# A linear-attention layer in four slots a chunk, with its convolution folded into the projection's weights, and one bias addition moved from ScalarE to VectorE

## The chip, the cores and the metric

The kernel runs on one core of one Trainium2 chip, as one launch. The metric is the time of that launch on the device, in microseconds (us); smaller is better. A core has five engines that run side by side, each through its own list of instructions in order: PE (TensorE, matrix products into PSUM banks), ACT (ScalarE), DVE (VectorE), POOL (GpSimd, which also issues the indirect DMAs) and SP (which issues the other DMAs). They wait for each other by semaphores.

## The reference

The program is a chain of sixteen layers on a tensor x of 16 sequences, 256 tokens and 128 features. Each layer adds its result on a normalized x to x. Two kinds of layer are touched by the change. The linear attention, cut to what it computes (`x` here is the normalized input):

```python
q = elu(x @ Wq.T) + 1
k = elu(x @ Wk.T) + 1
v = x @ Wv.T
kv = einsum('bhnd,bhne->bhde', k, v)              # 16 heads of 8
out = einsum('bhnd,bhde->bhne', q, kv)
den = maximum(einsum('bhnd,bhd->bhn', q, k.sum(tokens)), 1e-6)
xp = pad(x, one token on each side)
local = xp[:, :-2] * conv_w[:, 0] + xp[:, 1:-1] * conv_w[:, 1] + xp[:, 2:] * conv_w[:, 2] + conv_b
return (out / den + local) @ Wp.T + bp
```

The local layer (twice two of them in the program) is a windowed attention followed by a feed-forward part. Of the feed-forward part only its layer norm matters here: with h the token-shifted activations, `h = (h - mean) / sqrt(var + 1e-05) * lg + lb`, and `lb` is a bias for each feature.

## The kernel before

**Layout.** Features lie on the 128 partitions and tokens along the free dimension, all in 32-bit floats. The 4096 tokens are cut into 8 chunks of 512 tokens (two sequences each). x and the normalized activations h0 (the tile `ha`) stay in SBUF; the local layers hold a second tensor `hb`. Products go into 8 PSUM banks, which are handed out in turn, each by a `self.bank()`: a bank is used again once what was in it has been read.

**Slots.** `slots` (L1820) writes the order of a stage by hand. A stage is a list of steps; step i of chunk c is issued in slot `i + every * c`. Within a slot the later steps come first. The stage's own steps are followed by `last`, the first steps of the layer that comes next, which run on the chunks as they get done:

```python
for k in range((n - 1) * every + len(both)):
    ...
        for i in reversed(some):
            c, rest = divmod(k - i, every)
            if rest == 0 and 0 <= c < n and part < len(both[i]):
                both[i][part](c)
```

**The linear layer** (`linear`, L1966) has the steps: three of a norm (centre on PE; variance on PE and its root on ACT; scale on DVE), which chunks 0 to 4 have already behind them when the layer starts, since the layer before has run them ahead; `project` (q as one product 512 wide, k and v as eight 128 wide; then elu+1 of q and k: relu and exp on ACT, one step on DVE; and the convolution `l`, one step on ACT and two on DVE); `sums` (kv for two sequences, masked to its heads on DVE); `heads` (numerators and denominators on PE, then for each sequence a maximum, a reciprocal and a product on DVE); `join` (four transposes of o on PE, added to l on DVE); `out` (product with Wp, added to x on DVE). With `every=2` a chunk enters every second slot.

**What follows** is a mixture of experts. Its first steps (`Sending.steps`, L3644) are the `last` of the linear layer: three steps of a norm, `compare` (the gate's product on PE, comparisons on DVE), `choose` (DVE), `place` (small products on PE, DVE), `turn` (four transposes on PE, two copies on ACT) and `scatter`: eight indirect DMAs a chunk, issued by POOL, that write the rows of 128 tokens each to their places in DRAM (L3748). Before the first expert can run, SP fetches rows that these DMAs have written (L2165), together with the expert's weights (L2163). With `spread=False` all eight DMAs of a chunk are one step.

**The local layers' attention** (`local_attend`, L3363) has slots of its own, one for each half of a sequence's heads (32 in all; a chunk takes four). In each slot PE runs the score products, the products with v, transposes (`turn`), the value product, and two projections (`project`); ACT runs exponentials, copies out of PSUM, squares (sq), and the two small steps on `ss` that give each head's inverse length; DVE runs the four products `t` (rotary tables times the projections in PSUM), the minimum `pt` that masks the scores, the sum of squares and the division `ot`; POOL rotates (t<-t,t) and multiplies by the inverse lengths (t<-t,ss, 1.9 us). Three PSUM banks, tag "w", are shared by projections, transposes and the value product. Every fourth slot the output projection of a chunk (ps<-ot,w) comes in. Beside this `chunk_steps` (L3529) runs the norm of the feed-forward part for the chunks that are done: the four steps of `norm_of_half` (L3574), one a slot: centre, spread, scale (a DVE operation hb<-hb,w,nrs) and the bias (hb<-hb,w). In the slot of the bias, the steps are issued on DVE and ACT after `ot` and `ss` and before the `sq` and `t` of that slot's projection. The first layer of a local stage has one more step there for some chunks, the scale of the second layer's norm (ha<-ha,nrs on DVE).

**Helpers.** All operations go through short helpers, so that many have the line of a helper: `mm` L504 and `tr` L508 (PE), `act` L528 (ACT), `tt` L531, `ts` L538 and `stt` L543 (DVE), `gt` L534 (POOL).

Of the kernel before, what the change touches and what calls it, by code (L numbers as in the profile page):

```python
# [1649 lines left out]
class Fast(Net):  # L1650
# [313 lines left out]
            )  # L1964

    def linear(self, w):  # L1966
        x, h0 = self.x, self.ha
        nc = self.nc
        with ExitStack() as st:
            p = self.stage(st, "n2", 2)  # L1970
            qs, ks, kvs, os, ls = {}, {}, {}, {}, {}
            norm = [lambda c, i=i: self.norm_x_step(p, c, i) for i in range(3)]

            def elu1(ps, tag, bufs):
                e = p.tile([P, CH], F32, tag=tag, name=tag, bufs=bufs)
                self.act(e, ps, AF.Relu, scale=-1.0)
                self.act(e, e, AF.Exp, scale=-1.0)
                self.stt(e, ps, 0.0, e, ALU.max, ALU.add)
                return e

            def project(c):
                s = self.chunk(c)
                pq, pk, pv = self.bank(), self.bank(), self.bank()
                self.mm(pq, w["Wq"], h0[:, s])
                for t in range(4):
                    ht = h0[:, c * CH + t * P : c * CH + t * P + P]
                    self.mm(pk[:, t * P : t * P + P], ht, w["Wk"])
                    self.mm(pv[:, t * P : t * P + P], ht, w["Wv"])
                qs[c] = elu1(pq, "q", 3)
                k = elu1(pk, "k", 2)  # L1990
                v = p.tile([P, 4, P + 1], F32, tag="v", name="v")
                self.act(v[:, :, :P], pv.rearrange("p (t d) -> p t d", t=4), AF.Copy)
                nc.gpsimd.memset(v[:, :, P:], 1.0)
                ks[c] = k, v
                l = p.tile([P, CH], F32, tag="l", name="l", bufs=4)
                lb, hb = self.bt(l), self.bt(h0[:, s])
                self.act(l, h0[:, s], AF.Identity, scale=w["conv_w"][:, 1:2], bias=w["conv_b"])
                self.stt(lb[:, :, 1:], hb[:, :, : T - 1], w["conv_w"][:, 0:1], lb[:, :, 1:], ALU.mult, ALU.add)
                self.stt(lb[:, :, : T - 1], hb[:, :, 1:], w["conv_w"][:, 2:3], lb[:, :, : T - 1], ALU.mult, ALU.add)
                ls[c] = l  # L2000

            def sums(c):
                k, v = ks.pop(c)
                pkv = self.bank()
                for b in range(2):
                    for u in range(2):
                        t = 2 * b + u
                        self.mm(pkv[:, b * 129 : b * 129 + 129], k[:, t * P : t * P + P], v[:, t], start=u == 0, stop=u == 1)

                kv = p.tile([P, 2, P + 16], F32, tag="kv", name="kv")  # L2010
                src = pkv[:, :258].rearrange("p (b d) -> p b d", b=2)
                self.tt(kv[:, :, :P], src[:, :, :P], self.twice(self.k["blk8"]), ALU.mult)
                self.tt(kv[:, :, P:], src[:, :, P:].broadcast_to([P, 2, 16]), self.twice(self.k["blk8"][:, ::8]), ALU.mult)
                kvs[c] = kv

            def heads(c):
                q, kv = qs.pop(c), kvs.pop(c)
                o = p.tile([P, 4, P], F32, tag="o", name="o")
                for b in range(2):
# [4 lines left out]
                    src = pn[:, :288].rearrange("p (u d) -> p u d", u=2)  # L2024
                    rd = p.tile([P, 2, 16], F32, tag="rd", name="rd")
                    self.ts(rd, src[:, :, P:], 1e-6, ALU.max)
                    nc.vector.reciprocal(rd, rd)
                    self.tt(
                        o[:, 2 * b : 2 * b + 2].rearrange("p u (h d) -> p u h d", h=16),
                        src[:, :, :P].rearrange("p u (h d) -> p u h d", h=16),  # L2030
                        rd[:, :, :, None].broadcast_to([P, 2, 16, 8]), ALU.mult,
                    )
                os[c] = o

            def join(c):
                o, l = os.pop(c), ls[c]
                pt = self.bank()
                for t in range(4):
                    self.tr(pt[:, t * P : t * P + P], o[:, t])
                self.tt(l, l, pt, ALU.add)  # L2040

            def out(c):
                s = self.chunk(c)
                po = self.bank()
                self.mm(po, w["Wp"], ls.pop(c))
                self.stt(x[:, s], po, w["bp"], x[:, s], ALU.add, ALU.add)

            self.slots(NCH, *norm, project, sums, heads, join, out, last=self.lead(p), every=2)

    def mix(self, w):  # L2050

# [1536 lines left out]

    def local_ffn(self, w, z, hn, last):
# [261 lines left out]
```

## Time and profile before

| | us |
|---|---|
| median of 3 runs (4299.6, 4300.43, 4302.12) | 4300.43 |
| the profiled execution's own time | 4303.47 |
| its span in the profile | 4301.6 |
| linear layer: first projection to the first product of the experts | 1858.85 to 2011.31 |
| bias hb<-hb,w on ACT in the four attentions and feed-forward parts, one | 0.71 |

The busy shares over the whole span are 90% for PE, 61% DVE, 55% ACT and 49% POOL. In the timeline a line gives the start in us from the span's start, the duration in us, engine, source line, operation, output and inputs by tile names (buffer numbers left out), their shapes and how many equal ones are merged; in brackets stands the idle time before it and what ended it. A 32-bit matrix product shows as two records, so x2 is one product. Groups of instructions give the shortest, median and longest duration in ns. Windows give the busy time of each engine in a stretch, and behind them the clock that was granted to PE (1 is full) and the share of DMA engines in use.

### The profile page before, as it was taken

To read this page: it belongs to the slowest core of one execution; us is meant where nothing else is said; L and a number is where in the kernel's file an instruction comes from. 1 tells how busy PE (TensorE), PEld (TensorE's weight loads), DVE (VectorE), ACT (ScalarE), POOL (GpSimd) and SP (SyncE) were. 2 spreads that over 40 slices of the span, in tenths; PEclk is the share of its full clock that TensorE was granted. 3 is DMA by queue.
4 is the path that set the end of the run, shared out by engine and by line. 5 is a ranking of instruction groups with operands and counts; after the bars stand their busy time and mean duration, and the time that the engine had idled before them with its cause. 6 is when DMAs were issued, how large, how long until landed. Compare 5 with 4: busy or idle time off the path is not lost. (4 is left out here: it accounts for less than half of the span.)

```text
span 4301.6 us, 74012 instructions
## 1 busy us (share of the span) xinstructions
PE 3881.4 (90%) x28998; PEld 2210.2 (51%) x28998; DVE 2620.8 (61%) x4423; ACT 2369.4 (55%) x4821; POOL 2123.8 (49%) x1776
## 2 busy tenths in 40 slices
PE   7999999998899999985989879987999899899978
PEld 3555465465455466554955469543333343455333
DVE  4775576364577377464346633646888698386474
ACT  6665466555766466553456634454565544674432
POOL 4663465232565166226433334557988698421251
PEclk9999999988999999997999979998999999999989
DMA  1800000000000000004910068000000000000000
GB/s 60 339 2 1 11 2 1 19 1 1 20 1 2 3 2 1 1 6 147 321 60 15 18 213 272 18 18 16 1 1 1 3 0 1 15 2 18 6 0 21
DMA packets 78407, 176.45 MB, mean 41 GB/s; under 512 B 12607, under 2 KB 39109, under 8 KB 77921
## 3 DMA queue, kind: packets, MB, share of 16 engines
q1 hardware_dynamic: 65568, 148.40, 10.0%
q0 software_dynamic: 9120, 18.51, 1.2%
q8 instruction: 231, 3.78, 0.4%
q10 hardware_dynamic: 3360, 4.72, 0.3%
q14 instruction: 128, 1.04, 0.1%
HBM read 118.28 MB, written 54.20 MB: 40 GB/s over the span
## 5 line engine op out<-in xcount | busy, mean ns | idle before, releaser
L528 ACT ACTIVATE pt<-ps 128x512 f32<-128x512 f32 x640 | 339.7, 600 | 314.4 <-PE ps L504 313.1
L504 PE MATMUL ps<-hb,w 128*128 128x512 f32 (+1 forms) x960 | 464.4, 617 | 8.8 <-issue 3.3
L504 PE MATMUL ps<-w,hb 128*128 128x512 f32 (+2 forms) x896 | 405.5, 574 | 26.3 <-DVE t L531 20.4
L534 POOL TENSOR_TENSOR t<-t,t 128x512 f32<-128x512 f32 x256 | 319.6, 1270 | 161.5 <-DVE t L531 101.5
L531 DVE TENSOR_TENSOR t<-ps,tab 128x512 f32<-128x512 f32 x512 | 317.6, 681 | 84.9 <-ACT sq L528 81.5
L534 POOL TENSOR_TENSOR t<-t,ss 128x1024 f32<-128x1024 f32 x128 | 243.6, 1903 | 218.6 <-ACT ss L528 217.4
L504 PEld LDWEIGHTS ps<-hb,w 128*128 128x128 f32 (+1 forms) x960 | 180.0, 192 | 271.7 <-issue 239.8
L528 ACT ACTIVATE qkt<-ps 128x512 f32<-128x512 f32 x256 | 140.5, 595 | 309.6 <-PE ps L508 309.0
L531 DVE TENSOR_TENSOR ot<-ps,rd 128x512 f32<-128x512 f32 (+2 forms) x224 | 143.1, 639 | 254.3 <-ACT rd L528 254.3
L531 DVE TENSOR_TENSOR u<-u,ps 128x384 f32<-128x384 f32 (+1 forms) x206 | 121.8, 595 | 287.4 <-PE ps L508 186.1
L534 POOL TENSOR_TENSOR nsq<-ha 128x512 f32<-128x512 f32 x112 | 123.2, 1100 | 316.9 <-ACT ha L528 304.8
L504 PEld LDWEIGHTS ps<-w,hb 128*128 128x128 f32 x896 | 156.3, 193 | 184.4 <-issue 115.0
L504 PE MATMUL ps<-nsq,ct 128*128 128x512 f32 x368 | 203.0, 635 | 36.0 <-POOL nsq L534 32.1
L504 PE MATMUL ps<-ot,w 128*128 128x512 f32 x448 | 215.4, 615 | 16.8 <-DVE ot L531 9.0
L2199 POOL DMA_INDIRECT back<-y,x x142 | 139.1, 980 | 183.8 <-ACT y L528 68.0
L504 PE MATMUL ps<-u,w 128*128 128x512 f32 (+1 forms) x448 | 218.1, 611 | 8.3 <-POOL u L534 8.3
L504 PE MATMUL ps<-xt,w 128*128 128x128 f32 x1704 | 221.0, 280 | 1.5 <-ACT xt L528 1.5
L528 ACT ACTIVATE u<-ps,w 128x512 f32<-128x512 f32 x160 | 107.8, 685 | 183.2 <-PE ps L504 180.6
L531 DVE TENSOR_TENSOR pt<-pt,w 128x1024 f32<-128x1024 f32 (+1 forms) x96 | 181.1, 1886 | 42.7 <-ACT pt L528 42.7
L504 PEld LDWEIGHTS ps<-xt,w 128*128 128x128 f32 x1704 | 204.8, 194 | 2.9 <-ACT xt L528 2.9
L3748 POOL DMA_INDIRECT rows<-out,idx x128 | 125.9, 983 | 155.0 <-ACT out L528 105.7
L528 ACT ACTIVATE nrs<-ps,ct 128x512 f32<-128x512 f32 x208 | 139.8, 684 | 98.9 <-PE ps L504 93.1
(367 smaller groups left out, 9302.6 us busy)
## 6 DMA issues: line engine op xcount, KB each, us to landing
w<-in_moe_x SPq DMA_DIRECT2D x142, 533.0 KB
rows<-t SPq DMA_DIRECT2D x64, 520.0 KB
x<-rows SPq DMA_DIRECT2D x142, 65.0 KB
w<-in_local_f SPq DMA_DIRECT2D x8, 659.5 KB
y<-back ACTq DMA_DIRECT2D x16, 256.0 KB
y<-back SPq DMA_DIRECT2D x16, 256.0 KB
w<-in_local_f SPq DMA_DIRECT2D x4, 658.5 KB
back<-y,x POOLq DMA_INDIRECT x142
```

Of the source, the lines that this page charges most:

```text
L504: self.nc.tensor.matmul(out, lhsT, rhs, start=start, stop=stop)
L528: self.nc.scalar.activation(out, in_, func, **kw)
L531: self.nc.vector.tensor_tensor(out, a, b, op)
L534: self.nc.gpsimd.tensor_tensor(out, a, b, op)
L2199: nc.gpsimd.indirect_dma_start(views[i], bass.IndirectOffsetOnAxis(ap=x[:, C : C + 1].bitcast(I32), axis=0), y, None, bounds_check=2 * NT ...
L3748: nc.gpsimd.indirect_dma_start(views[(c * 2 + k) * 4 + t], bass.IndirectOffsetOnAxis(ap=idx[:, k, t : t + 1], axis=0), out[:, k, t], None,)
```

## The change

In the linear layer `every` goes from 2 to 4, and the elu's last DVE step becomes a step of its own, `grown`, a slot behind `project`. The convolution is no longer computed: the product with Wp of the shifted inputs is taken with three weight matrices, Wp scaled by each of the three taps, which are made once behind chunk 0's `grown`, together with a bias that holds `Wp conv_b + bp`. `join` now begins the output product of the chunk in its bank, with one product 512 wide and four 255 wide, and copies the transposed o out of PSUM on ACT; `out` adds the product of that copy to the same bank. In `heads` one reciprocal serves both sequences. The scatters of a chunk are four steps of two DMAs. In `norm_of_half`, which all four local layers use, the bias is added on DVE instead of ACT.

```diff
     def linear(self, w):
...
-            p = self.stage(st, "n2", 2)
+            one = self.stage(st, "n1", 1)
+            p = self.stage(st, "n2", 2)
...
+            taps = one.tile([P, 3, P], F32, tag="taps", name="taps")
+            bias = one.tile([P, 1], F32, tag="bias", name="bias")
+
+            def prepare():
+                for j in range(3):
+                    self.ts(taps[:, j], w["Wp"], w["conv_w"][:, j : j + 1], ALU.mult)
+                pb = self.bank()
+                self.mm(pb[:, :1], w["Wp"], w["conv_b"])
+                self.tt(bias, pb[:, :1], w["bp"], ALU.add)
...
-                qs[c] = elu1(pq, "q", 3)
-                k = elu1(pk, "k", 2)
+                made = []
+                for ps, tag in ((pq, "q"), (pk, "k")):
+                    e = p.tile([P, CH], F32, tag=tag, name=tag, bufs=3)
+                    self.act(e, ps, AF.Relu, scale=-1.0)
+                    self.act(e, e, AF.Exp, scale=-1.0)
+                    made.append((ps, e))
...
-                l = p.tile([P, CH], F32, tag="l", name="l", bufs=4)
-                lb, hb = self.bt(l), self.bt(h0[:, s])
-                self.act(l, h0[:, s], AF.Identity, scale=w["conv_w"][:, 1:2], bias=w["conv_b"])
-                self.stt(lb[:, :, 1:], hb[:, :, : T - 1], w["conv_w"][:, 0:1], lb[:, :, 1:], ALU.mult, ALU.add)
-                self.stt(lb[:, :, : T - 1], hb[:, :, 1:], w["conv_w"][:, 2:3], lb[:, :, : T - 1], ALU.mult, ALU.add)
-                ls[c] = l
+                ks[c] = made, v
+
+            def grown(c):
+                made, v = ks[c]
+                for ps, e in made:
+                    self.stt(e, ps, 0.0, e, ALU.max, ALU.add)
+                qs[c] = made[0][1]
+                ks[c] = made[1][1], v
+                if c == 0:
+                    prepare()
...
             def heads(c):
...
+                for b in range(2):
+                    self.ts(rd[:, b], srcs[b][:, :, P:], 1e-6, ALU.max)
+                nc.vector.reciprocal(rd, rd)
...
             def join(c):
-                o, l = os.pop(c), ls[c]
-                pt = self.bank()
+                o = os.pop(c)
+                hs = h0[:, self.chunk(c)]
+                pt, po = self.bank(), self.bank()
+                self.mm(po, taps[:, 1], hs, stop=False)
+                for b in range(2):
+                    at = b * T
+                    self.mm(po[:, at + 1 : at + T], taps[:, 0], hs[:, at : at + T - 1], start=False, stop=False)
+                    self.mm(po[:, at : at + T - 1], taps[:, 2], hs[:, at + 1 : at + T], start=False, stop=False)
                 for t in range(4):
                     self.tr(pt[:, t * P : t * P + P], o[:, t])
-                self.tt(l, l, pt, ALU.add)
+                ot = p.tile([P, CH], F32, tag="ot", name="ot")
+                self.act(ot, pt, AF.Copy)
+                pos[c] = po, ot
 
             def out(c):
                 s = self.chunk(c)
-                po = self.bank()
-                self.mm(po, w["Wp"], ls.pop(c))
-                self.stt(x[:, s], po, w["bp"], x[:, s], ALU.add, ALU.add)
-
-            self.slots(NCH, *norm, project, sums, heads, join, out, last=self.lead(p), every=2)
+                po, ot = pos.pop(c)
+                self.mm(po, w["Wp"], ot, start=False)
+                self.stt(x[:, s], po, bias, x[:, s], ALU.add, ALU.add)
+
+            self.slots(NCH, *norm, project, grown, sums, heads, join, out, last=self.lead(p, spread=True), every=4)
...
     def norm_of_half(self, pool, bank, w, s):
...
-            lambda: self.act(s, s, AF.Identity, bias=w["lb"]),
+            lambda: self.ts(s, s, w["lb"], ALU.add),
```

More of the change, by code (lines that the diff above doesn't have):

```diff
@@ L1969, in linear @@
         with ExitStack() as st:
+            one = self.stage(st, "n1", 1)
             p = self.stage(st, "n2", 2)
-            qs, ks, kvs, os, ls = {}, {}, {}, {}, {}
+            qs, ks, kvs, os, pos = {}, {}, {}, {}, {}
             norm = [lambda c, i=i: self.norm_x_step(p, c, i) for i in range(3)]
[L1974 to L1979, printed above, removed]
+            taps = one.tile([P, 3, P], F32, tag="taps", name="taps")
[6 more added lines that the diff above has]
+                self.tt(bias, pb[:, :1], w["bp"], ALU.add)
             def project(c):
@@ L1993, in project @@
                 nc.gpsimd.memset(v[:, :, P:], 1.0)
-                ks[c] = k, v
-                l = p.tile([P, CH], F32, tag="l", name="l", bufs=4)
-                lb, hb = self.bt(l), self.bt(h0[:, s])
-                self.act(l, h0[:, s], AF.Identity, scale=w["conv_w"][:, 1:2], bias=w["conv_b"])
-                self.stt(lb[:, :, 1:], hb[:, :, : T - 1], w["conv_w"][:, 0:1], lb[:, :, 1:], ALU.mult, ALU.add)
-                self.stt(lb[:, :, : T - 1], hb[:, :, 1:], w["conv_w"][:, 2:3], lb[:, :, : T - 1], ALU.mult, ALU.add)
-                ls[c] = l
+                ks[c] = made, v
[7 more added lines that the diff above has]
+                    prepare()
             def sums(c):
@@ L2018, in heads @@
                 o = p.tile([P, 4, P], F32, tag="o", name="o")
+                rd = p.tile([P, 2, 2, 16], F32, tag="rd", name="rd")
+                srcs = []
                 for b in range(2):
@@ L2023, in heads @@
                         self.mm(pn[:, u * 144 : u * 144 + 144], q[:, t * P : t * P + P], kv[:, b])
[L2024 to L2027, printed above, removed]
+                    srcs.append(pn[:, :288].rearrange("p (u d) -> p u d", u=2))
+                for b in range(2):
+                    self.ts(rd[:, b], srcs[b][:, :, P:], 1e-6, ALU.max)
+                nc.vector.reciprocal(rd, rd)
+                for b in range(2):
                     self.tt(
                         o[:, 2 * b : 2 * b + 2].rearrange("p u (h d) -> p u h d", h=16),
-                        src[:, :, :P].rearrange("p u (h d) -> p u h d", h=16),
-                        rd[:, :, :, None].broadcast_to([P, 2, 16, 8]), ALU.mult,
+                        srcs[b][:, :, :P].rearrange("p u (h d) -> p u h d", h=16),
+                        rd[:, b, :, :, None].broadcast_to([P, 2, 16, 8]), ALU.mult,
                     )
@@ L2035, in join @@
             def join(c):
-                o, l = os.pop(c), ls[c]
-                pt = self.bank()
+                o = os.pop(c)
+                hs = h0[:, self.chunk(c)]
+                pt, po = self.bank(), self.bank()
+                self.mm(po, taps[:, 1], hs, stop=False)
+                for b in range(2):
+                    at = b * T
+                    self.mm(po[:, at + 1 : at + T], taps[:, 0], hs[:, at : at + T - 1], start=False, stop=False)
+                    self.mm(po[:, at : at + T - 1], taps[:, 2], hs[:, at + 1 : at + T], start=False, stop=False)
                 for t in range(4):
                     self.tr(pt[:, t * P : t * P + P], o[:, t])
-                self.tt(l, l, pt, ALU.add)
+                ot = p.tile([P, CH], F32, tag="ot", name="ot")
+                self.act(ot, pt, AF.Copy)
+                pos[c] = po, ot
             def out(c):
                 s = self.chunk(c)
-                po = self.bank()
-                self.mm(po, w["Wp"], ls.pop(c))
-                self.stt(x[:, s], po, w["bp"], x[:, s], ALU.add, ALU.add)
-            self.slots(NCH, *norm, project, sums, heads, join, out, last=self.lead(p), every=2)
+                po, ot = pos.pop(c)
+                self.mm(po, w["Wp"], ot, start=False)
+                self.stt(x[:, s], po, bias, x[:, s], ALU.add, ALU.add)
+            self.slots(NCH, *norm, project, grown, sums, heads, join, out, last=self.lead(p, spread=True), every=4)
     def mix(self, w):
```

## The prediction

> **What bounds the kernel now.** I read the page first, for where TensorE (PE), the engine with 90% of the span, has holes; then windows around the changed stages; then the timelines there, engine by engine. The chain of waits covers only the last 6% of the span, far behind the change, so it says nothing here.
>
> ```profile
> span 4301.6 us, 74012 instructions
> ...
> PE   7999999998899999985989879987999899899978
> ...
> POOL 4663465232565166226433334557988698421251
> ```
>
> A slice is 107.5 us. The 5 in PE's row is slice 19, 1936 to 2043 us: the end of the linear layer. The slices from 110 to 1860 us, where the four local layers are, show 8 and 9. So the two edits meet different bounds.
>
> The linear layer, by windows (PE, PEld, DVE, ACT, POOL, clock, DMA), then its ends on POOL and PE:
>
> ```profile
> 1859.00:1922.00 63.00, 52.38 (x288) 37.06 (x287) 46.24 (x112) 33.83 (x59) 4.81 (x10) 0.95 0.01 1
> 1922.00:1981.00 59.00, 38.41 (x238) 25.78 (x237) 52.61 (x211) 29.41 (x56) 42.82 (x46) 0.87 0.20 61
> 1981.00:2011.00 30.00, 0.63 (x4) 0.35 (x4) 0.42 (x3) 0.00 (x0) 20.40 (x22) 0.50 0.22 70
> ```
> ```profile
> 1922.55 1.11 POOL L3748 DMA_INDIRECT rows<-out,idx  x1 [0.16 <-issue]
> ...
> 2006.83 0.97 POOL L3748 DMA_INDIRECT rows<-out,idx  x1 [0.31 <-issue]
> ```
> ```profile
> 2011.31 0.45 PE L508 MATMUL ps<-ct,x 128*128 128x128 f32 x1 [29.47 <-DMA x<-rows]
> ```
>
> In the last 30 us only POOL works: it issues the scatters that send the rows to the experts. There are 64, one each 1.27 us, 10.2 us a chunk; they begin at 1922.55 and end at 2007.8, and PE starts on the experts 3.5 us later. So the stage ends when POOL has issued its last scatter. Until 1950 DVE is 93% busy; projections of neighbouring chunks start 12.9 us apart (1921.83 and 1934.76).
>
> A local layer, one slot of the attention in which the bias is added:
>
> ```profile
> 616.70 0.69 DVE L531 TENSOR_TENSOR ot<-ps,rd 128x512 f32<-128x512 f32 x1 [2.30 <-ACT rd L528]
> 618.14 1.29 DVE L531 TENSOR_TENSOR t<-ps,tab 128x512 f32<-128x512 f32 x2 [0.76 <-ACT sq L528]
> ```
> ```profile
> 616.92 0.71 ACT L528 ACTIVATE hb<-hb,w 128x512 f32<-128x512 f32 x1
> ```
> ```profile
> 617.16 1.90 POOL L534 TENSOR_TENSOR t<-t,ss 128x1024 f32<-128x1024 f32 x1 [3.36 <-ACT ss L528]
> ```
> ```profile
> 619.67 1.09 PE L508 MATMUL ps<-ct,t 128*128 128x128 f32 x8
> 620.68 1.13 PE L504 MATMUL ps<-w,hb 128*128 128x512 f32 x2
> ```
>
> PE never rests here. But the value product at 620.68 writes the bank that the fourth product t (DVE, 618.14 to 620.62) has just read: PE is in time by nothing. Whatever delays t by more than 0.1 us delays PE.
>
> **The bias on DVE.** Removed: 32 ACT additions of 0.71 us (seven in each attention, one in each feed-forward part). Added: 32 DVE additions; the same operation in the performer gives the price, and its maximum a second one:
>
> ```profile
> L538 DVE TENSOR_SCALAR hb<-hb,w x8: 486/486/1151, 911.6 to 1046.8; 128x512 f32<-128x512 f32 x8
> ```
>
> The 1.15 us one began at 933.44 while a POOL operation ran (932.97 to 934.32); it ended 0.27 us after it. [...] This slot shows the same with another operation, in the cycles where the norm of a later chunk falls into it:
>
> ```profile
> 254.76 2.31 DVE L531 TENSOR_TENSOR ha<-ha,nrs 128x512 f32<-128x512 f32 x1
> ```
> ```profile
> 258.32 0.66 PE L508 MATMUL ps<-ct,t 128*128 128x128 f32 x4 [0.54 <-DVE t L531]
> 259.52 1.12 PE L504 MATMUL ps<-w,hb 128*128 128x512 f32 x2 [0.54 <-DVE t L531]
> ```
>
> It takes 0.68 us elsewhere, and here waits for POOL's product (254.62 to 256.53), as 20 of the 40 scale steps hb<-hb,w,nrs do: (61.5 us - 40 x 0.74) / 1.56 = 20. PE pays: from the slot's output projection to the next centring it takes 13.01 us without such an operation (608.63 to 621.64) and 14.39 with one (246.09 to 260.48), and the cycle of four slots grows from 34.35 (608.63 to 642.98) to 35.72 (322.01 to 357.73). That is 1.38 us a time, not won back.
>
> The moved addition stands in the same place, behind ot and ahead of the four t. It can issue at 617.31 (ot's start plus 0.61); POOL's product starts at 617.16, set by ACT's ss, which does not move. So it waits until 0.19 us ahead of that product's end (as ha did: 2.31 - 0.74 = 1.57 us after 254.76), 618.87, and ends at 619.36; t starts at 619.28 instead of 618.14. Queued behind it: four t, the minimum for the softmax, the sum of squares; PE waits for t. It costs 1.38 less the shorter operation (0.74 - 0.49), 1.13 us. Projections and t run only in five of a layer's seven bias slots, so 20 times. In six of these (chunks 1 to 3 in the first layer of each local stage) ha has waited already: the addition adds 0.41, or 0.77 if the POOL copy that follows goes first; I take 0.6. Sum: 14 x 1.13 + 6 x 0.6 = **+19.4 us**. The other twelve stand where no t follows: nothing, as DVE idles over half of those parts (feed-forward: 21.17 of 55 us). Bounds: never held, t starts 0.4 us earlier and the 0.08 us that PE waits now goes, 20 x -0.08 = -2; held at ha's price, 14 x 1.38 + 6 x 0.77 = +24.
>
> A rule speaks for this edit: the Trainium skill, Perfetto Trace Analysis, "Optimizing Scalar/DVE Operations", has an operation that Scalar or DVE can do run faster on DVE if a performance mode exists, unless DVE is saturated. By its word the edit is worth 32 x (0.49 - 0.71) = -7 us at most; the rows above decide against it.
>
> **The linear layer.** DVE loses, a chunk, two convolution steps (1.44 us start to start), the join (0.60) and one of two reciprocals (0.33): 12.9 - 2.4 = 10.5 us. ACT loses 0.80 and gains a 0.6 copy of ot. Prepare: three 128x128 scalings, some 0.2 us each, one tiny product, one tiny addition, before the first kv: hidden behind PE's first sums. PE gains the taps:
>
> ```profile
> 2899.13 1.88 PE L504 MATMUL ps<-ha,Wr 128*128 128x512 f32 x6
> 2900.85 1.45 PE L504 MATMUL ps<-ha,Wk 128*128 128x512 f32 x4
> ```
>
> One group there is a 512-wide product and two 255-wide: 1.72 us, so 0.86 and 0.43 each; the taps are 0.86 + 4 x 0.43 = 2.58 us a chunk. The slot with the projection now holds taps, transposes of o, projection and turn: 6.1 us of PE. The other three are chains. In us from a projection's start, by start-to-start times of the 1920 to 1936 timeline: projection 2.64, turn 0.44, out issued at 3.08, x on DVE at 4.18, q 4.84, k 5.44, sums on PE 0.84 behind k at 6.28, kv 7.45, choose 7.90, its 'both' done and place on PE at 9.62, mean 9.82, taps 10.76, transposes 13.34, next projection **13.8**. PE idles 1.4 us before sums and waits again for 'both'. With the norm of chunks 5 to 7 PE fills that: 6.28 + 0.97 + 0.94 + 0.86 + 0.98 + 0.20 + 0.94 + 2.58 + 0.43 = **14.2**. The fill: chunk 0 to 1 is 11.1 (sums at 5.04 as now, kv 6.27, heads 6.85 to 7.9, taps 2.7, transposes 0.43), then 13.1 and 13.4 (no turn yet). So the last projection stands at 11.1 + 13.1 + 13.4 + 13.8 + 3 x 14.2 = 94 us, plus 2 for the clock, which falls to 0.58 in the present fill (1873 to 1878) for idle gaps like these: 1858.85 + 96 = 1954.9, where it is 1934.76 now.
>
> The first scatter comes in the slot of the fourth projection, 37.6 + 4.9 = 42.5 us in (turn, then ACT's backlog, then a 0.5 us copy): 1901.4 instead of 1922.55. But a period of 14 is longer than POOL's 10.2, so POOL waits from chunk to chunk until chunk 4, turned beside the last projection: 1954.9 + 4.9 = 1959.8. From there chunks 4 to 7 need 4 x 10.2 = 40.8 us without a gap (5 is turned 13.8 us later, 6 and 7 follow each within 10): end at 2000.6, against 2007.8: **-7.2 us**. Scatters in pairs cost POOL nothing, as only memsets and three nsq (1.04 us) stand between. SP's order is unchanged; its row fetch follows POOL's end as now. Bounds: POOL never waiting after its first scatter, 1901.4 + 81.6 = 1983, -24.8; periods of 15.5 from the third on and another 4 us of half clock, +3.
>
> Sum: +19.4 - 7.2 = **+12.2 us**. The profiled execution took 4303.47 (span 4301.6, 1.9 around it), 3 above the median; the median becomes 4300.4 + 12.2 = **4312.6**.
>
> **The rivals.** First, other side: the addition is not held. It misses POOL's product by 0.15 us; if it starts first, POOL waits 0.49 us and nobody waits for POOL. Against it: ha and the scale step miss by the same 0.14 and are held all 20 times. Time 4300.4 - 7.2 - 1.6 = 4291.6; it decides once fewer than 7 of the 20 are held. Second: the linear chains overlap better, POOL runs saturated: 4300.4 + 19.4 - 24.8 = 4295. For it: PE's and DVE's work (11.9, 10.5) would allow 12; against it: the chain above. Third: the fold makes PE the bound, with the clock low: the linear layer 5 us slower, 4325. For it: PE's 2.6 us a chunk; against it: PE still idles 0.5 to 1.9 us in each period.
>
> **How the numbers follow.** Forecast 0.55 (own range 4304 to 4320), first rival 0.18, second 0.12, third 0.15. A measurement here tells 0.2% (8.6 us) from no change: below 4291.8, above 4309.0. Faster: six tenths of the first and a third of the second, 0.15. Same: the rest of these and a fifth of the forecast, 0.26. Slower: 0.59. The range 4291 to 4321 leaves out half of the first rival and two thirds of the third.
>
> **What would show it.** The bias row on DVE near 2.0 us where its price is 0.49; PE behind t 20 times more; the clean cycle at 35.5 instead of 34.35; the linear layer starting 19 us later. In it: projections 13.8 to 14.2 apart, first scatter 42 us behind the first projection, POOL gapless over the last four chunks, PE's hole of 29.5 us down to about 20. A bias row of 0.5 us, or scatters gapless from the first, would prove me wrong.

## The result and the profile after

The changed kernel takes 4320.58 us (median of 6 runs, 4314.88 to 4327.27), the kernel before 4301.45 us (6 runs): a ratio of 1.0042, 95% interval 1.0032 to 1.0052. It is 19.1 us slower. The profiled execution took 4322.03 us (span 4320.2), against 4303.47 (span 4301.6). The 18.6 us between the spans come about so: 21.3 were lost when the linear layer starts (first projection at 1880.17 instead of 1858.85), 20.0 of them in the local layers and 1.3 ahead of them; the linear layer gave 4.4 back (148.04 us from there to the experts' first product, instead of 152.46); another 1.7 were lost behind it. No edit touches the stretches that lost the 1.3 and the 1.7.

The page of the changed kernel, its span and its slices of 108 us:

```profile
span 4320.2 us, 74143 instructions
...
PE   7999999998899999997989879987999899899977
...
POOL 4654365232565166325433444457988699411251
```

Slice 19 of PE's row, the linear layer's, went from 5 to 7. The slices of the local layers still show 8 and 9, and the loss is in there: a digit of a tenth doesn't show the 3% by which a cycle grows. The group of the moved addition, which had x8 at a median of 486 ns, does:

```profile
L538 DVE TENSOR_SCALAR hb<-hb,w x40: 473/826/2044, 219.5 to 1836.1; 128x512 f32<-128x512 f32 x40
```

The timeline of one slot in the second local layer, the one the prediction showed, on DVE, POOL and PE:

```profile
624.41 0.69 DVE L531 TENSOR_TENSOR ot<-ps,rd 128x512 f32<-128x512 f32 x1 [2.30 <-ACT rd L528]
624.88 1.90 POOL L534 TENSOR_TENSOR t<-t,ss 128x1024 f32<-128x1024 f32 x1 [3.35 <-ACT ss L528]
625.02 2.04 DVE L538 TENSOR_SCALAR hb<-hb,w 128x512 f32<-128x512 f32 x1
626.98 2.47 DVE L531 TENSOR_TENSOR t<-ps,tab 128x512 f32<-128x512 f32 x4
628.31 0.66 PE L508 MATMUL ps<-ct,t 128*128 128x128 f32 x4 [0.47 <-DVE t L531]
629.51 1.12 PE L504 MATMUL ps<-w,hb 128*128 128x512 f32 x2 [0.54 <-DVE t L531]
```

POOL's product runs from 624.88 to 626.78; the addition is issued 0.14 us behind its start, stands for 2.04 us instead of 0.48, and ends 0.28 us after it. The first t starts 2.57 us behind ot, where it was 1.44. PE, which had waited for nothing here, waits 0.47 us for the transposes' input and 0.54 for the bank of the value product. The cycle of four slots grows from 34.35 to 35.44 us. These are the output projections that begin and end it, in the kernel before and in the changed one:

```profile
608.63 3.70 PE L504 MATMUL ps<-ot,w 128*128 128x512 f32 x8
642.98 3.70 PE L504 MATMUL ps<-ot,w 128*128 128x512 f32 x8
```

```profile
616.36 3.70 PE L504 MATMUL ps<-ot,w 128*128 128x512 f32 x8
651.80 3.70 PE L504 MATMUL ps<-ot,w 128*128 128x512 f32 x8
```

The linear layer by windows (PE, PEld, DVE, ACT, POOL, clock, DMA), and its ends on POOL and PE:

```profile
1880.00:1943.00 63.00, 54.59 (x296) 39.98 (x295) 33.41 (x106) 28.32 (x52) 12.62 (x17) 0.95 0.04 10
1943.00:2002.00 59.00, 53.57 (x293) 37.67 (x291) 40.58 (x152) 31.38 (x58) 38.21 (x42) 0.94 0.17 54
2002.00:2028.00 26.00, 3.80 (x24) 3.06 (x24) 7.84 (x38) 4.05 (x7) 17.39 (x18) 0.50 0.25 73
```

```profile
1925.37 1.10 POOL L3771 DMA_INDIRECT rows<-out,idx  x1 [24.14 <-DVE x L543]
2023.66 0.96 POOL L3771 DMA_INDIRECT rows<-out,idx  x1 [0.30 <-issue]
```

```profile
2028.21 0.45 PE L508 MATMUL ps<-ct,x 128*128 128x128 f32 x1 [14.76 <-DMA x<-rows]
```

DVE falls from 46.2 to 33.4 us in the first 63, PE rises from 52.4 (0.83) to 54.6 and in the second window from 38.4 to 53.6: the bound has moved from DVE to PE, which works 13.9 us of each of the last three periods of 14.6. The first scatter comes 45.2 us behind the first projection (63.7 before), the last 143.5 us behind it (148.0 before). Only 4.5 of the 18.5 us by which POOL starts earlier are left at its end: before chunk 4 it waits for the projections, which are now 13 to 14.6 us apart.

### The profile page after: what moved, and what is told of

It reads as the page before. It is cut to its first block, busy times and chain, and to the rows that moved or that the text cites. A ratio compares the mean times of both kernels' runs of the same rounds, so it can differ in the third digit from the quotient of the medians.

```text
span 4320.2 us, 74143 instructions
## 1 busy us (share of the span) xinstructions
PE 3902.2 (90%) x29080; PEld 2232.0 (52%) x29080; DVE 2639.1 (61%) x4427; ACT 2350.3 (54%) x4789; POOL 2127.0 (49%) x1776
## 5 line engine op out<-in xcount | busy, mean ns | idle before, releaser
L504 PE MATMUL ps<-hb,w 128*128 128x512 f32 (+1 forms) x960 | 464.5, 617 | 9.4 <-issue 3.3
L504 PE MATMUL ps<-w,hb 128*128 128x512 f32 (+2 forms) x896 | 406.2, 575 | 35.4 <-DVE t L531 28.4
L504 PEld LDWEIGHTS ps<-hb,w 128*128 128x128 f32 (+1 forms) x960 | 180.5, 193 | 273.2 <-issue 241.2
L504 PEld LDWEIGHTS ps<-w,hb 128*128 128x128 f32 x896 | 156.8, 194 | 196.2 <-issue 113.9
L504 PE MATMUL ps<-ot,w 128*128 128x512 f32 x464 | 222.9, 613 | 17.1 <-DVE ot L531 9.0
L504 PE MATMUL ps<-nsq,ct 128*128 128x512 f32 x368 | 200.3, 627 | 34.0 <-POOL nsq L534 29.1
L504 PE MATMUL ps<-u,w 128*128 128x512 f32 (+1 forms) x448 | 217.6, 609 | 8.0 <-POOL u L534 8.0
L504 PE MATMUL ps<-xt,w 128*128 128x128 f32 x1704 | 219.8, 279 | 1.5 <-ACT xt L528 1.5
L504 PEld LDWEIGHTS ps<-xt,w 128*128 128x128 f32 x1704 | 203.6, 193 | 2.8 <-ACT xt L528 2.8
```

The costliest lines, as they stand in the source:

```text
L504: self.nc.tensor.matmul(out, lhsT, rhs, start=start, stop=stop)
```

## The experiments

They ran on three chips (on which one the first comparison ran is not on record), where the kernel before takes 4325.4 us (the first four below), 4298.6 (the next four) and 4321.1 (the last four). Every ratio is to the kernel before on the same chip; it is estimated from all runs of both kernels and differs from the quotient of the medians by up to 0.0007. "Local" is the stretch from the first output projection of the first local layer to the first projection of the linear layer, "linear" the stretch from there to the experts' first product, both from the one profiled execution, which can lie some us off the median.

| kernel | median us | ratio, 95% interval | local us | linear us |
|---|---|---|---|---|
| before (first comparison) | 4301.45 | 1 | 1683.3 | 152.5 |
| changed (first comparison) | 4320.58 | 1.0042, 1.0032 to 1.0052 | 1703.3 | 148.0 |
| bias alone on DVE | 4347.70 | 1.0052, 1.0038 to 1.0066 | 1703.1 | 165.3 |
| linear layer alone | 4322.85 | 0.9994, 0.9985 to 1.0003 | 1683.1 | 158.0 |
| bias on DVE, early | 4312.61 | 0.9977, 0.9968 to 0.9986 | 1668.3 | 166.2 |
| slots without the fold | 4317.68 | 0.9981, 0.9972 to 0.9990 | 1684.5 | 157.1 |
| changed, bias early | 4289.90 | 0.9982, 0.9973 to 0.9991 | 1675.4 | 148.2 |
| no bias in the attention | 4294.25 | 0.9988, 0.9979 to 0.9997 | 1675.5 | 152.1 |
| fold without the slots | 4302.17 | 1.0004, 0.9995 to 1.0013 | 1685.0 | 152.5 |
| changed, bias early, x last | 4282.95 | 0.9970, 0.9958 to 0.9982 | 1671.9 | 144.8 |
| slots without fold, bias early | 4305.93 | 0.9964, 0.9953 to 0.9975 | 1668.6 | 155.1 |
| the same, x last | 4308.29 | 0.9970, 0.9960 to 0.9981 | 1675.5 | 156.0 |
| changed, bias early, no spreading | 4311.97 | 0.9981, 0.9970 to 0.9991 | 1668.6 | 161.7 |
| changed, bias early, x last, again | 4313.23 | 0.9980, 0.9970 to 0.9990 | 1671.9 | 158.9 |

On the first and the last of these three chips the linear layers are longer, on the first shown for the unchanged one too (165 instead of 152 us; more in the last section), so "linear" is compared within a group of four alone. "Local" moves by up to 7 us with PE's clock in the stage between the two local stages, which no edit touches; the cycles given below are free of that.

### One edit at a time

The bias alone, everything else as before:

```diff
-            lambda: self.act(s, s, AF.Identity, bias=w["lb"]),
+            lambda: self.ts(s, s, w["lb"], ALU.add),
```

> The kernel before, with the bias of norm_of_half on DVE and nothing else. If the addition is held by POOL's product and delays the four t (the forecast's mechanism), this edit alone costs all that the local part lost: +19 to +22 us (4321 to 4324), bias row near 2.04 us, cycle 35.44 instead of 34.35 us. If the loss belongs to the two edits together, or the bias is harmless, the time stays within 4299 to 4304. If the falls of PE's clock in the local part come from the longer waits, they are here at the same cycles (40.39 and 38.16 us); if they come with something else of the changed kernel, they are gone and the cost is near +16.

It costs 22 us (1.0052), and its local part is as long as the changed kernel's to 0.2 us. The addition's row is 473/827/2041 ns, the cycle 35.45 us, and the fall of PE's clock comes again (a cycle of 40.39 us in the second stage). So the loss is this edit's alone.

The linear layer alone is the changed kernel with that line put back:

> The changed kernel with the bias back on ACT. If the linear layer gains the 4.4 us that its two times show, 4297; cycles of the local part at 34.35 us again, first projection at 1858.9, first period 13.9 us. If the first period (13.9 us where 11.1 was forecast) was a lower clock left over from the local part, the first period falls to about 11 to 12 and the time to 4294. If the linear layer's gain was only bought with a pause that the bias gave it, 4301.

0.9994 with an interval that holds both 1 and the -4.4 us of the two profiles: not to be told from no change. Local is 1683.1 us again. The first period fell to 10.92 us, as the second theory had it, but the time did not follow, because on this chip the periods from the fifth projection on are 16.5 to 17.6 us instead of 14.6. Beside the unchanged linear layers of this group, 165.3 us with the bias alone and 166.2 with the early addition, its 158.0 is still 7 to 8 us shorter; in the profiled execution 3.8 us of that are lost ahead of the first local layer (first output projection at 180.27 us, at 176.49 and 176.48 in those two), where no edit works. The changed kernel with an early bias had a first period of 13.88 us without any loss in its local part, so what the longer stalls of the local part leave behind isn't its cause. PE's clock in this period itself is; the changed kernel, then this one:

```profile
1880.17:1894.04 13.87, 11.36 (x51) 8.87 (x50) 5.61 (x15) 2.96 (x6) 1.85 (x4) 0.75 0.02 1
```

```profile
1863.36:1874.28 10.92, 8.40 (x52) 6.62 (x51) 5.62 (x15) 2.95 (x6) 1.84 (x4) 1.00 0.03 2
```

PE is busy 2.96 us longer at a clock of 0.75, which is the whole difference. Why the clock fell in the one and not in the other is open.

### Where the addition stands

The same 32 additions on DVE, but in the attention issued ahead of `ot`:

```diff
+                    c, rest = divmod(m - 9, 4)
+                    if rest == 0 and 0 <= c < NCH - 1:
+                        steps[1][3]()
                     if within(m - 1, NTILE):
                         inverse(m - 1)
                         divide(m - 1)
...
-                for i in range(4):
+                for i in range(3):
                     if (c := due(6 + i)) is not None and c < NCH - 1:
```

> The kernel before with the same 32 additions on DVE, but in the attention each is issued ahead of ot instead of behind it, where DVE and POOL both rest. If it is the meeting with POOL's product that costs, the bias row falls to about 0.49 us, no t starts late, and the time is that of before: 4300 to 4303. If an added DVE operation in this slot costs wherever it stands (DVE's own length, or what DVE does behind it), 4311 to 4322.

Faster than before, by 10 us (0.9968 to 0.9986), where no change was expected. The same slot on DVE and POOL, and the group:

```profile
613.08 0.17 DVE L531 TENSOR_TENSOR ss<-ss,least 128x16 f32<-128x16 f32 x1
613.18 0.48 DVE L538 TENSOR_SCALAR hb<-hb,w 128x512 f32<-128x512 f32 x1
615.55 0.69 DVE L531 TENSOR_TENSOR ot<-ps,rd 128x512 f32<-128x512 f32 x1 [1.90 <-ACT rd L528]
616.39 0.69 DVE L531 TENSOR_TENSOR t<-ps,tab 128x512 f32<-128x512 f32 x1
```

```profile
616.01 1.91 POOL L534 TENSOR_TENSOR t<-t,ss 128x1024 f32<-128x1024 f32 x1 [3.35 <-ACT ss L528]
```

```profile
L538 DVE TENSOR_SCALAR hb<-hb,w x40: 473/480/1150, 216.1 to 1800.7; 128x512 f32<-128x512 f32 x40
```

The addition takes 0.48 us in a gap of DVE and ends 2.35 us before POOL's product begins. The first t starts 0.84 us behind ot, where it was 1.44 before the change and 2.57 with it. This shows that the meeting with POOL's product makes the addition dear, not the addition. The cycle is 33.96 us, 0.39 below that of before. That is so in the fourteen cycles without ha; the six with it stay as long as they were. Where it comes from shows on ACT, in the kernel before and then in this one:

```profile
616.57 0.45 ACT L528 ACTIVATE ss<-ss 128x16 f32<-128x16 f32 x2
616.92 0.71 ACT L528 ACTIVATE hb<-hb,w 128x512 f32<-128x512 f32 x1
617.53 1.06 ACT L528 ACTIVATE sq<-ps 128x512 f32<-128x512 f32 x2
618.49 0.45 ACT L528 ACTIVATE pu<-ps 128x128 f32<-128x128 f32 x2
```

```profile
615.43 0.45 ACT L528 ACTIVATE ss<-ss 128x16 f32<-128x16 f32 x2
615.78 1.06 ACT L528 ACTIVATE sq<-ps 128x512 f32<-128x512 f32 x2
616.73 0.45 ACT L528 ACTIVATE pu<-ps 128x128 f32<-128x128 f32 x2
```

Before, two things stood behind the addition on ACT: sq, which t waited 0.76 us for, and the copies pu, which begin 1.92 us behind ss there and 1.30 us here. PE's products of that slot take 1.96 us from the first to the transposes before (617.71 to 619.67), 1.76 here (616.57 to 618.33); the rest of the 0.39 us are two steps of PE behind t, 0.08 and 0.10 us shorter. To see whether it is ACT's addition and nothing else, the attention's additions were left out on both engines:

```diff
-                for i in range(4):
+                for i in range(3):
                     if (c := due(6 + i)) is not None and c < NCH - 1:
```

> The kernel before without the addition of lb in the four attentions, on either engine (chunks 0 to 6; the one in the feed-forward part stays). If the 0.39 us a cycle that the early addition won is ACT's 0.71 us, which stood between ss and the sq that t's next work waits for, the cycle is 33.96 us here too and the time that of the early addition, within 2 us. If DVE's early addition won it in another way (by delaying ot, so that DVE and POOL fall into another order), the cycle stays at 34.35 us and the time at that of before.

The cycle is 33.97 us: ACT's addition had cost 0.39 us a cycle, and an early one on DVE costs nothing. Local is 7.8 us shorter than before: 5.3 in fourteen cycles, 1.6 for a fall of PE's clock in the third local layer that did not come, 0.9 in the first feed-forward part, which the edit doesn't touch. The ratio, 0.9988, is nearer to 1 than that of the early addition on the other chip, for two reasons outside the edit: the stretch between the two local stages, where the early addition had 6.9 us of luck with PE's clock, is as long here as before, and the first local layer starts 3.2 us later than before.

The changed kernel with this place for the addition:

> The changed kernel whole, with the 32 additions still on DVE, but in the attention ahead of ot instead of behind it. If the place alone made the bias dear, both edits now gain: the local part's 7 to 8 us (cycle 33.96 us) and the linear layer's 2 to 4 us, 9 to 12 us below the kernel before, ratio 0.9972 to 0.9979. If what the early addition gained in its own run was only a luckier clock in the stages between the local layers (6.6 us of its 15 there), it is 3 to 5 us below, ratio near 0.999.

0.9982: 8.7 us below the kernel before. In the profiles local is -7.9 (5.5 of it in the cycles) and linear -4.2: there both edits gain. The profiles' sum, 12.1 us, lies just beyond the interval's far end (11.6).

### The linear layer's parts

The fold in the old order (two slots a chunk, the elu whole in `project`, eight scatters in one step):

```diff
+                    self.stt(e, ps, 0.0, e, ALU.max, ALU.add)
                     made.append((ps, e))
...
-            self.slots(NCH, *norm, project, grown, sums, heads, join, out, last=self.lead(p, spread=True), every=4)
+            self.slots(NCH, *norm, project, sums, heads, join, out, last=self.lead(p, spread=False), every=2)
```

> The changed linear layer in the old order: the fold, the one reciprocal and the copy of ot, but two slots a chunk, the elu's last step back in the projection's step and eight scatters in one step; bias on ACT. If DVE bounds the old order (12.9 us a chunk) and the fold takes 2.4 us of it, periods fall to about 11.5 to 12 (PE then works 11.9), the last projection comes 5 to 7 us earlier than before and the linear layer ends 5 to 7 us earlier: ratio near 0.9985. If PE binds at once, because taps and transposes stand in one slot with the projection, periods stay at 13 or above and the time is that of before or 2 to 5 us over it.

Nothing: 1.0004, linear 152.52 us against 152.46. The last projection stands 76.85 us behind the first, 75.9 before. The window of its last projections shows why (columns as above):

```profile
1913.00:1953.00 40.00, 39.07 (x245) 29.36 (x243) 31.32 (x117) 24.20 (x45) 19.35 (x24) 1.00 0.09 30
```

DVE has fallen to 78%, and PE is busy 98% of the time: what the fold takes from DVE, PE gets, and PE has no more to give. The other half, slots without the fold, puts the convolution back on ACT and DVE and leaves the rest of the changed linear layer:

```diff
-                self.mm(po, taps[:, 1], hs, stop=False)
...
-                ot = p.tile([P, CH], F32, tag="ot", name="ot")
-                self.act(ot, pt, AF.Copy)
-                pos[c] = po, ot
+                self.tt(l, l, pt, ALU.add)
...
+                l = p.tile([P, CH], F32, tag="l", name="l", bufs=3)
...
+                self.act(l, h0[:, s], AF.Identity, scale=w["conv_w"][:, 1:2], bias=w["conv_b"])
```

> The changed kernel with the bias on ACT and the convolution on ACT and DVE as it was (no taps on PE, no copy of ot): four slots a chunk, grown, one reciprocal and scatters in pairs stay. If PE sets the period of 14.6 us (13.9 of it are busy) and the fold is what fills it, the period falls by most of the taps' 2.6 us to 12.0 to 12.5, the last projection comes 14 to 17 us earlier, and POOL, which then works almost without a gap, ends 14 to 18 us earlier: 4280 to 4284. If DVE becomes the bound when the convolution and the join come back (2.0 us a chunk), the period stays at 14 or more and the time is 4296 to 4303.

0.9981, 8 us below before, but not the 14 to 18 expected: linear 157.1 us, within 1 us of the linear layer alone with the fold (158.0) on the same chip. The mean period of 14.2 us is what the second theory said, but not for its reason: DVE is busy for 84.9 of the first 120 us. Without the fold PE waits instead: the periods are 11.7 to 18.8 us, and its granted clock falls to 0.67 to 0.84 in five of eleven windows of 10 us. With the early addition it was tried on another chip:

> The early addition, and the linear layer in four slots a chunk with the convolution as it was before on ACT and DVE: no taps, no copy of ot. Where no stalls come from outside, PE's period loses the taps' 2.6 us and the last projection comes 8 to 12 us earlier than with the fold, so that POOL issues almost without a gap: linear layer 136 to 141 us where it is 148.2 with the fold, ratio to before 0.995 to 0.9965. If the chain over DVE takes their place (convolution and join back on DVE, 2.0 us a chunk), the linear layer stays at 146 to 150 us and the ratio at 0.998.

> The same with the update of x behind q and k. If the chain over x, q, k, sums holds the period there as it does with the fold, another 3 to 4 us off: linear layer 133 to 138 us, ratio 0.994 to 0.996. If DVE or POOL sets the period, within 1.5 us of the kernel without it.

> The changed kernel with the early addition and x behind q and k, once more beside the two kernels without the fold on one chip: linear layer 144.8 us, ratio 0.997. If the fold costs PE more than it brings DVE, it is 6 to 12 us behind them; if not, level with them or ahead.

The second edit of these is "x last": the update of x on DVE issued behind q and k, by making `out` two parts of a step.

```diff
-                self.stt(x[:, s], po, bias, x[:, s], ALU.add, ALU.add)
+            def added(c):
+                s = self.chunk(c)
+                self.stt(x[:, s], pos.pop(c)[0], bias, x[:, s], ALU.add, ALU.add)
...
-            self.slots(NCH, *norm, project, grown, sums, heads, join, out, last=self.lead(p, spread=True), every=4)
+            self.slots(NCH, *norm, project, grown, sums, heads, join, (out, added), last=self.lead(p, spread=True), every=4)
```

On that chip the kernel without the fold stands at 0.9964, with x last too at 0.9970, with the fold and x last at 0.9980: 7 and 5 us apart in the medians, and the intervals overlap. Linear was 155.1, 156.0 and 158.9 us, far from the 133 to 145 expected, since the later periods are longer there (up to 19.2 us). So the fold brings nothing there and may cost some us; that it costs 6 to 12 is not confirmed, and on a chip without those delays the kernel without the fold was not tried. Putting x last brought nothing to the kernel without the fold. To the one with it, it brought something in the profile, on the chip without delays:

> The changed kernel with the early addition, and in the linear layer the update of x on DVE behind the steps of q and k instead of ahead of them. If the chain projection, turn, out, x, q, k, sums sets the period, sums on PE start 0.6 us earlier, the period falls from 14.6 to about 14.0 us and the linear layer ends 3 to 5 us earlier than with the early addition alone. If PE is the bound (13.9 of 14.6 us busy) or sums wait for another thing than k, the gain is under 1 us.

```profile
1847.34 1.02 PE L504 MATMUL ps<-ha,w 128*128 128x512 f32 x2
...
1865.98 1.13 PE L504 MATMUL ps<-v,k 128*128 128x129 f32 x8 [1.08 <-DVE k L543]
...
1942.48 1.02 PE L504 MATMUL ps<-ha,w 128*128 128x512 f32 x2
...
1992.09 0.45 PE L508 MATMUL ps<-ct,x 128*128 128x128 f32 x1 [16.96 <-DMA x<-rows]
```

These are the first projection, the second chunk's sums, the last projection and the experts' first product: 144.75 us in all, 3.5 less than with x first, as expected. The sums' wait for k fell from 2.13 to 1.08 us. But the gain is in the second to fourth period (11.89, 12.81, 13.02 us against 12.95, 14.44, 13.77), and the 14.44 holds a fall of PE's clock that the changed kernel didn't have there (13.24), so some 1.2 us of the 3.5 aren't the edit's. The last three stay at 14.51 (14.62 before that edit): there PE is the bound, not the chain. At 0.9970 (0.9958 to 0.9982) and 4282.95 us this is the lowest of that group and clear of the kernel before, but its interval overlaps that with x first (0.9973 to 0.9991), and half of the 7 us between their medians lies in the local part of the profiles (1671.9 and 1675.4), which is the same in both kernels. On the third chip it stands at 0.9980, beside 0.9981 with x first and the scatters in one step. So that x last makes the kernel faster is not shown by the times.

Last, the scatters of a chunk in one step:

> The changed kernel with the early addition, but the eight scatters of a chunk in one step as before. If scatters in pairs cost and bring nothing (only memsets and three nsq stand between), the linear layer takes 147 to 150 us as with pairs, ratio 0.998. If eight in a row delay POOL's nsq for the norm of chunks 5 to 7 (10 us behind a chunk's scatters), periods of the last projections grow and the layer takes 5 to 15 us longer, ratio 0.9995 to 1.002.

0.9981 against 0.9982 with pairs: no difference in time that these runs tell. Linear, 161.7 us, stands on the chip with the delays, without a partner there that differs in this alone, so the profile doesn't decide.

## Why the prediction was right

**The whole.** Forecast +12.2 us, measured +18.6 between the spans. The time of 4320.58 us lies a little above the forecast's own range (4304 to 4320) and just within the whole one (4291 to 4321). The 6.4 us between forecast and measurement are 0.6 in the local part, 2.8 in the linear layer, and 3.0 in the stretches ahead of the one and behind the other that no edit touches.

**The addition's price.** Forecast +19.4 us, with the row near 2.0 us, t 1.14 late and 1.13 a time in 14 slots. Measured: 2.04 us, 1.13 late (2.57 against 1.44), 1.09 a time, in fourteen slots as forecast. In the six slots with ha before it, it cost 0.74 where I took 0.6 (its row there 0.83 us, with POOL's copy ahead of it: the bound's upper end). 14 x 1.09 + 6 x 0.74 = 19.7. The rest is PE's clock, which the sum had not. Three falls behind the longest waits added 1.7 each, 5.1. Two falls that the kernel before has, at the end of the attention in the first layer of each stage, didn't come, 1.6 each, 3.2. The cycle of chunk 4 in the first of these layers, before and changed, at clocks of 0.95 and 1.00:

```profile
357.73:392.68 34.95, 32.44 (x336) 20.77 (x332) 21.09 (x35) 20.42 (x54) 15.45 (x13) 0.95 0.01 2
```

```profile
365.76:400.20 34.44, 30.94 (x336) 19.93 (x332) 22.95 (x36) 19.90 (x53) 15.63 (x13) 1.00 0.01 2
```

So this cycle got 0.5 us shorter with the addition in it; in the third layer, where the fall of before comes a cycle later, the same cycle grows from 33.34 to 34.44, as elsewhere. With 0.9 less in the first feed-forward part and 0.7 less between the stages, 19.7 + 5.1 - 3.2 - 0.9 - 0.7 is the measured 20.0. The price came out for its own reason, and the early addition shows the mechanism; that the changes of the clock nearly cancel is luck.

**The first rival** was priced wrongly. I gave an addition that isn't held -1.6 us, and as bound -2, from the 0.08 us that PE visibly waited behind t. It is -0.39 us in each of fourteen cycles, -5.5, because two more of PE's steps hung on ACT's addition, through the copies pu behind sq. It is nothing in the six cycles with ha.

**The rule weighed in the prediction** (the Trainium skill, Perfetto Trace Analysis, "Optimizing Scalar/DVE Operations") came to -7 us by its word, and the kernels with the early addition gained 5.5 in cycles. It held for the engine (0.48 us instead of 0.71); the place decided whether it could. That the figures are near each other is chance: what counts is fourteen times 0.39 us of cycle, not 32 times a difference of two durations.

**The linear layer.** Forecast -7.2, measured -4.4. Its steps: last projection at +96 (measured 97.7), chunk 4's scatters 4.9 behind it (5.1), then 40.8 us without a gap (41.7, one gap of 1.2 for ACT's copy). Two terms of the projections were mis-sized. The last three periods came as 14.6 instead of 14.2, 1.2 us in all. The fill, first to second projection, took 13.87 us where the sum had 11.1 and 2 more for the clock: at full clock it takes 10.92 (the linear layer alone), so the 11.1 was right and the clock's part is 2.9. The others came as 12.9, 13.2 and 13.8 for 13.1, 13.4 and 13.8. PE's hole fell from 29.5 to 14.8 us, further than the 20 forecast: PE's last product ahead of it ends 35.6 us behind the last projection, where the forecast's times leave 29.

**The other rivals.** POOL was not saturated. The fold did make PE the bound (98% in the fold alone), as the third rival had it, but without making the layer slower: in the old order what it cost PE came to as much as what it saved DVE (the layer took 152.52 us with it and 152.46 without).

## What to carry to other kernels

When an operation changes its engine, read what is issued around it there: this one cost 20 us behind `ot`, and ahead of it the cycles became 5.5 us shorter, for the same instruction. Look for it in the gap of the engine that it moves to, and check that the neighbour which can hold it rests in that gap. And price what an engine is freed of by everything queued behind it, not by the one wait that ends in sight.

## What the runs showed of the hardware

**Who comes second is held for the rest of the first's operation.** DVE's addition, issued 0.14 us behind POOL's product, stood for 2.04 us instead of 0.48; the product itself kept its 1.90 us. The Trainium skill, SBUF — State Buffer, "Who interferes with whom", states such a lock for the ports that these two engines share, held for the whole instruction by the one that issues first. The row agrees, but for 0.28 us: the addition ended that much after POOL's recorded end, which is less than its own 0.48. Not every operation of DVE is held. The sum of squares reads and writes SBUF alone, and it took 1.21 us within an operation of POOL, in the kernel before:

```profile
620.80 2.49 POOL L534 TENSOR_TENSOR t<-t,t 128x512 f32<-128x512 f32 x2 [0.41 <-PE ps L508]
621.47 1.21 DVE L3410 TENSOR_REDUCE ss<-sq 128x16 f32<-128x1024 f32 x1
```

It takes the same 1.21 us at 250.44, between two operations of POOL (one ends at 250.44, the next starts at 254.62).

**PE's clock fell behind waits of 2.02 us in a cycle in which PE is 93% busy.** The cycle from 287.21 to 327.60 us in the first local layer, changed kernel, by windows and on PE:

```profile
290.00:300.00 10.00, 8.57 (x89) 5.35 (x87) 6.72 (x8) 5.66 (x15) 5.36 (x6) 1.00 0.01 2
300.00:310.00 10.00, 9.27 (x81) 5.33 (x81) 7.48 (x13) 5.17 (x14) 5.99 (x7) 0.83 0.00 0
```

```profile
298.05 0.66 PE L508 MATMUL ps<-ct,t 128*128 128x128 f32 x4
300.19 0.66 PE L508 MATMUL ps<-ct,t 128*128 128x128 f32 x4 [1.48 <-DVE t L531]
301.38 2.04 PE L504 MATMUL ps<-w,hb 128*128 128x512 f32 x2 [0.54 <-DVE t L531]
303.21 1.85 PE L504 MATMUL ps<-hb,ct 128*128 128x512 f32 x2
```

From 298.05 to 301.38 PE runs eight transposes and waits 2.02 us; the products behind it take 2.04 and 1.85 us instead of 1.12 and 1.02, and the cycle is 1.7 us longer. It happened in three of the six slots of this form, at the same cycles in the run with the bias alone in the second stage; before the change, with waits of 0.54 and 0.54, in none. Longer waits alone don't decide it: the kernel before has a fall of its own at the end of each of the four attentions, behind waits of 0.80 and 0.79 us in the first, and in the changed kernel two of the four are gone. The Trainium skill, TensorE: Matmul & The Clock Gate, "Why this matters for your kernels", warns of idle gaps above some 3 us; no single gap here is that long, and whether the transposes count as idle was not tried.

**One program, two chips.** The changed kernel with the early addition and x last, its transposes of o and their reader on ACT, on the second chip and on the third:

```profile
1898.51 0.60 PE L508 MATMUL ps<-ct,o 128*128 128x128 f32 x4
1899.15 0.60 ACT L528 ACTIVATE ot<-ps 128x512 f32<-128x512 f32 x1 [1.67 <-PE ps L508]
```

```profile
1900.50 0.60 PE L508 MATMUL ps<-ct,o 128*128 128x128 f32 x4
1903.75 0.60 ACT L528 ACTIVATE ot<-ps 128x512 f32<-128x512 f32 x1 [4.28 <-PE ps L504]
```

The copy starts 0.64 us behind the start of its transposes on the one, 3.25 us on the other, with all else in step until then. On the two chips where the kernel before takes over 4320 us this delay (1 to 4 us, also of DVE's `l<-l,ps`) comes back chunk by chunk while POOL scatters, and lengthens the linear layer by 10 to 14 us (158.0 for 148.0, 166.2 for 152.5, 158.9 for 144.8). The trace puts the end of the long wait down to a later product of PE (ps L504), though in the same program on the other chip the wait ended with the transposes. Why stays open, and so does whether it is the chip or the hour, which differ together.
